# One quarter of the scan's inputs built by TensorE instead of GpSimd, with the scan tiles' partitions reordered and the schedule rewritten

## The chip, the cores and the metric

The kernel runs on one core of one Trainium2 chip. The metric is the device time of one execution in microseconds. The engines are named as in the profile: PE (TensorE; PEld is its weight loading), DVE (VectorE), ACT (ScalarE), POOL (GpSimd) and SP (SyncE, which here issues nearly all DMAs).

## The reference, cut to what matters

The input x is [32, 96, 56, 56]. Layer 0 is an inverted bottleneck of convolutions with a squeeze-and-excite gate; the change does not touch it. Layer 1 runs two Mamba blocks over the 3136 positions of each image, then a fusion, a batch norm and a residual. A Mamba block is:

```
xs, z = split(layernorm(seq) @ in_w)                # 192 channels each
xc    = silu(causal_conv(xs, 4 taps))
dt, B, C = split(xc @ xproj_w)                      # 6, 16 and 16 columns
delta = softplus(dt @ dt_w + dt_b)                  # [L, 192]
dA    = exp(delta[..., None] * A)                   # [L, 192, 16]
dBx   = delta[..., None] * B[:, :, None, :] * xc[..., None]
h     = scan: h_t = dA_t * h_(t-1) + dBx_t          # along L
y     = einsum('blds,bls->bld', h, C) + Dp * xc
out   = seq + (y * silu(z)) @ out_w
```

So each of 192 channels carries 16 states, and the largest arrays are dA, dBx and h with 192 x 16 rows of 3136 positions for each of 32 images and two blocks.

## The kernel before, in words

Layer 1 cuts each image into `NQ` = 4 chunks of `LC` = 784 positions: 128 chunks and two blocks, 256 *units* in all (`units`, L581). The work of a unit is `NT` = 24 *positions* `t`. At each position DVE scans a tile of 128 partitions x 784: 32 channels times 4 states. `place(t)` gives its block of 64 channels `k` (0 to 2), its group of four states `j` (0 to 3) and its half `p` of the block. The two positions with the same `k` and `j` are a *pair*; a unit has 12 pairs. A tile's partition is channel x 4 + state.

The main loop (the end of the phase, in `manual_schedule`) writes the order of all engines by hand. For each position `at` of the long sequence of 256 x 24 positions it emits, in this order:

- `inject(at + 4)`, once a pair: POOL multiplies u = delta * xc of the pair with B into `bx` (128 x 1568, L877), two pairs ahead of its scan;
- `decay(at + 1)`: ACT writes dA = exp(delta * A) (128 x 784, L857) into one of two PSUM buffers `da` of two banks each. So the exp for one position needs the buffer that the scan two positions earlier has given back;
- `bring(at)`, once a pair: ACT copies the first `LP` = 512 columns of C to PSUM as `cp` (L865);
- bursts in `early` (an activation that needs another function table: table load L590, the activation, table load back L591);
- `gated` (DVE, L941), `scan(at)` (DVE, L889), `product` (DVE multiplies h of the pair before by `cp`, columns 0 to 511, L897), `rest` (POOL does the other 272 columns, L904);
- `reduce(at - 5)`: PE sums h * C over the four states into `y` by matmuls with `rel` (L930);
- the steps that `prepare` and `finish` have put at this position: they make the inputs of the next unit (layer norm, the convolution by PE into `xs` L690, gate `z` L706, `bc` L715, `dt` L727, delta, u), and project a finished one (L789, L793);
- `fetch`: SP issues the loads that repeat rows over partitions, eight or nine positions ahead: delta and u (each row to 4 partitions) and B and C (4 rows to 32 channels each), all from scratch in DRAM that the unit's own steps have written (L722, L734).

Every engine works through its queue in this order, so a step of PE that waits holds up all PE work behind it. Banks for the steps' results come from a pool of two (`bank`), so a matmul step also waits until ACT or DVE has emptied the bank used two steps before. The delta activation (softplus), the silu of xc and the silu of z are three separate bursts in a unit. Block 1 works two chunks behind block 0 (`units`).

Of the kernel before, what the change touches and what calls it, by code (L numbers as in the profile page):

```python
# [11 lines left out]
F32 = mybir.dt.float32  # L12
# [15 lines left out]
LP = 512  # L28
# [9 lines left out]
ROUND = 12582912.0  # L38

# [14 lines left out]
def conv_mamba_kernel(ctx, tc, a, out):  # L54
# [397 lines left out]
    with ExitStack() as ph:  # L452
# [28 lines left out]
        v.tensor_reduce(rel, eye.rearrange("p (m s) -> p m s", s=SN), AX.X, ALU.add)  # L481
# [14 lines left out]
        move = once.tile([128, SG, DG, SN], F32, name="move", tag="move")  # L496
        v.tensor_copy(move, eye.rearrange("p (j s d) -> p j d s", j=SG, s=SN))
        acol = wts.tile([128, SG, NL, 2 * NB], F32, name="acol", tag="acolb")
        ps = bank("acol")
        for j in range(SG):  # L500
            for m in range(DB // DG):
                pe.matmul(
                    ps[m * 32 : m * 32 + 32, j * NL * 2 * NB : (j + 1) * NL * 2 * NB], move[:, j].rearrange("p d s -> p (d s)"),
                    araw[:, :, m :: DB // DG], start=True, stop=True,
                )
# [66 lines left out]
        g.memset(xn[C : C + 1, :], 1.0)  # L572
        tails = [wts.tile([C + 1, KC - 1], F32, name=f"tail{i}", tag=f"tail{i}") for i in range(NL)]
# [7 lines left out]
        units = [(0, 0), (1, 0)]  # L581
        for c in range(2, nch):
            units += [(c, 0), (c - 2, 1)]
        units += [(nch - 2, 1), (nch - 1, 1)]
# [3 lines left out]
        def through(t, func):  # L588

            s.activation(t, t, func)  # L590
            s.preload_act_table_set(MAIN)  # L591
# [6 lines left out]
        def prepare(n):  # L598
# [9 lines left out]
            def load():  # L608
                if i == 0:
                    seqs[c, 0] = wt([C, LC], "seq0", 3, n)  # L610
                    sp.dma_start(seqs[c, 0], x1d[b][:, q * LC : (q + 1) * LC])
# [5 lines left out]
            def square(h):  # L617
                if h == 0:
                    d["sq"] = wt([C, LC], "sq", 1, n)
                s.activation(d["sq"][:, cols(h)], d["cen", h][:C, :HB], AF.Square)  # L620
# [38 lines left out]
            def normalise(m):  # L659
                if m == 0:  # L660
                    d["xt"] = wt([TK, NK, C], "xt", 1, n)
                for k in TURNS[m]:
                    o = (k - TURNS[m][0]) * C
                    s.activation(d["xt"][:, k, :], d["ct", m][:TK, o : o + C], AF.Copy, scale=d["rs"][:, k : k + 1])  # L664
# [70 lines left out]

            def softplus():
                through(d["dl"], AF.Softplus)
                spread("delta", d["dl"], slice(0, NB))
# [16 lines left out]
            late, then = (9, 4) if n in (3, len(units) - 1) else (0, 0)  # L755
            steps = [(-4, load)]
            for h in range(2):
                steps += [(-1 + h + late, lambda h=h: center(h)), (-1 + 1 + h + late, lambda h=h: square(h))]
            steps += [(-1 + 2 + late, variance), (-1 + 3 + late, root), *[(t + late, lambda m=m: newton(m)) for m, t in enumerate((2, 2, 3))]]
            for h in range(2):  # L760
                steps += [(7 + h + then, lambda h=h: turn(h)), (8 + h + then, lambda h=h: normalise(h))]
                steps += [(9 + h + then, lambda h=h: turn_back(h)), (10 + h + then, lambda h=h: normal(h))]
            steps += [(11 + 3 + then, trail)]
            for k in range(NB):
                t = (12, 14, 16)[k] + then
                steps += [(t, lambda k=k: conv(k, (0, 1))), (t + 1, lambda k=k: conv(k, (2, 3)))]
                steps += [((14, 16, 18)[k] + then, lambda k=k: keep("xc", 3, "xs", k))]
            steps += [(18.5 + then, lambda: through(d["xc"], AF.Silu)), (20 + then, project_bc), (21 + then, store_bc)]
            for k in range(NB):
                steps += [((17, 19, 21)[k] + then, lambda k=k: gate(k)), ((18, 20, 22)[k] + then, lambda k=k: keep("z", 3, "zp", k))]  # L770
                steps += [((22, 22, 23)[k] + then, lambda k=k: project_dt(k)), ((23, 23, 24)[k] + then, lambda k=k: keep("dl", 1, "dtp", k))]
            steps += [(26.5 + then, lambda: through(d["z"], AF.Silu)), (34.5 + then, softplus), (35 + then, lambda: input_u(NB - 1))]
            steps += [(34 + then, lambda: bring_x(0)), (36 + then, lambda: input_u(0))]
            steps += [(38 + then, lambda: bring_x(1)), (39 + then, lambda: input_u(1))]
            return steps

        def finish(n):
# [17 lines left out]
            def store(h):  # L795
                if i + 1 < NL:
                    if h == 0:
                        seqs[c, i + 1] = wt([C, LC], f"seq{i + 1}", 3, n)
                    s.copy(seqs[c, i + 1][:, cols(h)], d["o", h][:C, :HB])
                    return  # L800
                if h == 0:
                    d["pre"] = wt([C, LC], "pre", 1, n)
                at = 2 * c + h
                s.activation(
                    d["pre"][:, cols(h)], d["o", h][:C, :HB], AF.Identity, bias=g2[:, b : b + 1],
                    accum_out=stats[:, 0, at : at + 1],
                )
                if at == 0:
                    s.activation(pivot, stats[:, 0, 0:1], AF.Copy, scale=-1.0 / HB)
                squares = wt([C, HB], "squares", 1, at)  # L810
                s.activation(squares, d["pre"][:, cols(h)], AF.Square, bias=pivot, accum_out=stats[:, 1, at : at + 1])

            def count():
# [5 lines left out]
                (4, lambda: [project(k) for k in (None, 0, 1)]), (5, lambda: project(2)),  # L819
                (6, lambda: store(0)), (7, lambda: store(1)), (8, count),  # L820
            ]

        LAG = 5
# [5 lines left out]
        def fetch(at, tags):  # L829

            n, t = divmod(at, NT)
            if not 0 <= n < len(units):
                return
            k, j, p = place(t)
            d = data[n]
            for tag in tags:
                if tag in ("delta", "u"):
                    if j == 0:
                        if p == 0:
                            d[tag, k] = wt([128, 2, LC], f"{tag}b", 2, f"{n}_{t}")  # L840
                        to = d[tag, k][:, p, :]
                        c0 = DB * (2 * k + p)
                        sp.dma_start(to, d[tag][c0 : c0 + DB, :].unsqueeze(1).to_broadcast([DB, SN, LC]))
                elif k == 0 and p == 0:
                    to = d[tag, j] = wt([128, LC], tag, 4 if tag == "B" else 5, f"{n}_{t}")
                    c0 = "BC".index(tag) * NS + j * SN
                    sp.dma_start(to, d["bc"][c0 : c0 + SN, :].unsqueeze(0).to_broadcast([DB, SN, LC]))

        das, bxs, hhs, hcs, cps, yps = {}, {}, {}, {}, {}, {}

        def decay(at):

            n, t = divmod(at, NT)
            i, d = units[n][1], data[n]
            k, j, p = place(t)
            das[at] = dpool.tile([128, 2 * 512], F32, name=f"da_{at}", tag="da")
            s.activation(das[at][:, :LC], d["delta", k][:, p, :], AF.Exp, scale=acol[:, j, i, 2 * k + p : 2 * k + p + 1])  # L857
# [13 lines left out]
        def inject(at):  # L871
# [3 lines left out]
            if p == 0:  # L875
# [5 lines left out]
        def scan(at):  # L881
# [4 lines left out]
            if p == 0:  # L886
                hhs[at] = wt([128, 2, LC], "hh", 3, at)
                hcs[at] = wt([128, 2, LC], "hc", 4, at)
            v.tensor_tensor_scan(  # L889
                hhs[at - p][:, p, :], das.pop(at)[:, :LC], bxs.pop(at), state[i][:, t : t + 1] if c % NQ else 0.0,  # L890
# [8 lines left out]
        def rest(at):  # L899
# [3 lines left out]
            if p == 1:  # L903
                g.tensor_mul(hcs[at - 1][:, :, LP:], hhs[at - 1][:, :, LP:], beside(data[n]["C", j][:, LP:]))  # L904
# [40 lines left out]
        for n in reversed(range(len(units))):  # L945
            for t, step in prepare(n):
                (todo if t % 1 == 0 else early).setdefault((n - 2) * NT + math.ceil(t), []).append(step)
            for t, step in finish(n):
                todo.setdefault((n + 1) * NT + t, []).append(step)

        s.preload_act_table_set(MAIN)
        with tc.manual_schedule():
            for at in range(min(todo), total + NT):
                if 0 <= at + 4 < total:
                    inject(at + 4)
                if 0 <= at + 1 < total:
                    decay(at + 1)
                if 0 <= at < total:
# [11 lines left out]
                if 0 <= at < total:  # L970
                    rest(at)
                if 0 <= at - LAG < total:
                    reduce(at - LAG)
                for step in todo.get(at, ()):
                    step()
                fetch(at + 8, ("delta", "u", "C"))
                fetch(at + 9, ("B",))

# [78 lines left out]
```

## Time and profile before

The times are 18930.19, 18954.67 and 18966.92 us, median 18954.67 us. The profiled execution spans 18935.6 us, which is 19 us (0.1%) below the median.

| what | value |
|---|---|
| span of the profiled execution | 18935.6 us |
| layer 1, from the first `y` matmul to the last | 3449.0 to 18640.9 us |
| DVE / POOL / ACT / PE busy share of the span | 93 / 81 / 77 / 79% |
| the same in layer 1 (8000 to 14000 us) | 98 / 99 / 86 / 78% |
| granted PE clock, whole span | 0.829 |
| DMA, mean | 140 GB/s; 0.51 of the engines' time in layer 1 |

How to read it: layer 0 takes the first fifth of the span and is not touched. In layer 1 the pattern of a unit repeats 256 times, so what counts is the time of one unit. A busy share is only a bound on how much an engine could be relieved; which engine is waited for is read from the waits. PE's busy time covers also the modelled tails of its matmuls and stretches at half clock, so it overstates how full PE is. A matmul of 32-bit numbers leaves two records in the trace.

### The profile page before, as it was taken

The page shows a single profiled execution, that of the slowest core. Times are in us where ns is not written, and L with a number is a line of the kernel's source. Part 1 is how long each engine was busy: PE and PEld are TensorE (multiplying, and loading weights), DVE is VectorE, ACT ScalarE, POOL GpSimd, SP SyncE. Part 2 cuts the span into 40 slices and gives each one's busy share as a digit, 9 for nine tenths or more (in the row PEclk, how much of TensorE's full clock was granted, in tenths as well). Part 3 has the DMA queues.
Part 4 walks back from the last instruction along what each step waited for, and adds up shares of the span by engine and source line. Part 5 has one row for each costly group of instructions (what it writes and reads, how often), then busy time and mean ns, then how long its engine had stood idle before and what let it go on. Part 6 is the DMA issues. An engine that isn't in the chain of part 4 may idle for free.

```text
span 18935.6 us, 291237 instructions
## 1 busy us (share of the span) xinstructions
PE 15002.3 (79%) x109276; PEld 6041.9 (32%) x109276; DVE 17699.9 (93%) x13147; ACT 14621.6 (77%) x24492; POOL 15355.8 (81%) x6638
## 2 busy tenths in 40 slices
PE   8999998777777777777777777777777777777772
PEld 4545444322222222222222222222222222222220
DVE  8888888799999999999999999999999999999993
ACT  4444444688888888888888888888888888888884
POOL 0000000799999999999999999999999999999994
PEclk9999999788888888888888888888888888888885
DMA  1010100455555554555555555555555555555557
GB/s 30 26 27 22 27 23 21 129 164 164 164 164 164 164 163 163 163 163 164 164 164 164 164 164 164 164 163 163 163 163 163 164 164 164 164 164 164 164 163 208
DMA packets 1049777, 2641.91 MB, mean 140 GB/s; under 512 B 130424, under 2 KB 343632, under 8 KB 1042216
## 3 DMA queue, kind: packets, MB, share of 16 engines
q1 hardware_dynamic: 1039720, 2584.68, 42.4%
q0 software_dynamic: 6656, 38.54, 1.0%
q8 instruction: 856, 14.02, 0.3%
q14 instruction: 561, 4.60, 0.1%
q10 hardware_dynamic: 1984, 0.07, 0.0%
HBM read 2172.52 MB, written 449.58 MB: 138 GB/s over the span
## 4 chain that ended last, share of the span: by engine, by line
issue 36%; DVE 27%; ACT 18%; PE 9%; POOL 7%; DMA 2%; SPq 0%; DVEq 0%; POOLq 0%; ACTq 0%
DVE hc L897 12%; DVE hh L889 12%; ACT da L857 5%; PE xs L690 5%; POOL bx L877 4%; ACT L590 3%; ACT L591 2%; DVE h L308 2%; ACT cp L865 2%; POOL hc L904 2%; DMA C<-bcd 1%; ACT z L590 1%; PE y L930 1%; ACT z L701 1%; ACT xc L590 1%
## 5 line engine op out<-in xcount | busy, mean ns | idle before, releaser
L877 POOL TENSOR_TENSOR bx<-ub,B 128x1568 f32<-128x1568 f32 x3072 | 10943.8, 3562 | 117.1 <-DMA ub<-ud 68.7
L889 DVE TENSOR_TENSOR_SCAN hh<-da,state,bx 128x784 f32<-128x784 f32 x4608 | 8301.2, 1836 | 196.1 <-ACT da L857 189.7
L857 ACT ACTIVATE da<-deltab,acol 128x784 f32<-128x784 f32 x6144 | 5592.6, 915 | 869.6 <-DVE hh L889 820.0
L904 POOL TENSOR_TENSOR hc<-hh,C 128x544 f32<-128x544 f32 x3072 | 4168.2, 1357 | 76.2 <-DVE hh L889 67.8
L690 PE MATMUL xs<-xn,wx 97*64 97x392 f32 x12288 | 2813.0, 611 | 1284.8 <-DVE us L751 1284.8
L897 DVE TENSOR_TENSOR hc<-hh,cp 128x1024 f32<-128x1024 f32 x3072 | 3669.0, 1194 | 0.1
L930 PE MATMUL y<-hc,rel 128*32 128x392 f32 x24576 | 2979.8, 568 | 29.0 <-DVE hc L897 17.3
L889 DVE TENSOR_TENSOR_SCAN hh<-da,bx 128x784 f32<-128x784 f32 x1536 | 2681.0, 1776 | 160.9 <-ACT da L857 145.9
L383 POOL TENSOR_TENSOR x<-x,x 96x784 f32<-96x784 f32 x128 | 286.3, 2237 | 3044.5 <-ACT x L382 2968.6
L308 DVE SCALAR_TENSOR_TENSOR h<-hpad,hp,h 128x1568 f32<-128x1568 f32 x1024 | 2036.5, 1989 | 34.2
L690 PEld LDWEIGHTS xs<-xn,wx 97*64 97x64 f32 x12288 | 995.6, 165 | 3074.3 <-DVE us L751 1531.9
L865 ACT COPY cp<-C 128x512 f32<-128x512 f32 x3072 | 1784.7, 581 | 230.4 <-DVE hc L897 207.9
L715 PE MATMUL bc<-xc,wbc 64*64 64x392 f32 x3072 | 878.1, 728 | 542.5 <-ACT xc L590 542.5
L282 PE MATMUL dw<-hpad,diag 32*32 32x392 f32 x36864 | 1101.0, 514 | 46.9 <-issue 45.9
L671 PE MATMUL xn<-eye,xt 112*96 112x112 f32 (+1 forms) x4096 | 743.6, 350 | 433.6 <-ACT xt L664 432.3
L701 ACT COPY xc<-xs 128x392 f32<-128x392 f32 x768 | 372.1, 485 | 915.6 <-PE xs L690 915.6
L930 PEld LDWEIGHTS y<-hc,rel 128*32 128x32 f32 x24576 | 542.0, 114 | 1456.1 <-issue 1287.7
L590 ACT ACT_TABLE_LOAD x768 | 985.3, 1283 | 13.5
L591 ACT ACT_TABLE_LOAD x768 | 985.3, 1283 | 11.3
L380 PE MATMUL c<-h,w3s 128*96 128x392 f32 (+1 forms) x2560 | 958.3, 519 | 36.9 <-DVE w3s L365 36.9
L793 PE MATMUL o<-z,outw 64*96 64x392 f32 x3072 | 862.4, 699 | 96.4 <-DVE z L941 96.2
L289 ACT ACTIVATE h<-dw,turn 128x392 f32<-128x392 f32 x512 | 340.1, 673 | 731.8 <-PE dw L282 731.8
(172 smaller groups left out, 17257.0 us busy)
## 6 DMA issues: line engine op xcount, KB each, us to landing
deltab<-deltad SPq DMA_DIRECT2D x1536, 392.0 KB, 5.7
ub<-ud SPq DMA_DIRECT2D x1536, 392.0 KB, 5.9
B<-bcd SPq DMA_DIRECT2D x1024, 392.0 KB, 6.8
C<-bcd SPq DMA_DIRECT2D x1024, 392.0 KB, 5.2
deltad<-dl SPq DMA_DIRECT2D x512, 294.0 KB, 3.4
ud<-us SPq DMA_DIRECT2D x512, 196.0 KB, 2.8
ud<-us SPq DMA_DIRECT2D x512, 98.0 KB, 2.9
x<-in_x_dram SPq DMA_DIRECT2D x32, 1176.0 KB, 7.7
```

The source lines that it names most:

```text
L282: pe.matmul(ps[r][to : to + 32, :HB], diag[src, n, t, :], hb[src, r0 : r0 + RB, dx : dx + W], start=t == 0, stop=t == 8, skip_group_check= ...
L308: v.scalar_tensor_tensor(acc, src, tap, acc, ALU.mult, ALU.add)
L590: s.activation(t, t, func)
L591: s.preload_act_table_set(MAIN)
L690: pe.matmul(d["xs", k][h * 64 : h * 64 + 64, :HB], wx[:, i, o, k * 64 : k * 64 + 64], xn[:, o + h * HB : o + h * HB + HB], start=o == 0, s ...
L857: s.activation(das[at][:, :LC], d["delta", k][:, p, :], AF.Exp, scale=acol[:, j, i, 2 * k + p : 2 * k + p + 1])
L865: s.copy(cps[at], data[n]["C", j][:, :LP])
L877: g.tensor_mul(bx, data[n]["u", k], beside(data[n]["B", j]))
L889: v.tensor_tensor_scan(hhs[at - p][:, p, :], das.pop(at)[:, :LC], bxs.pop(at), state[i][:, t : t + 1] if c % NQ else 0.0, ALU.mult, ALU.add,)
L897: v.tensor_mul(hcs[at - 1][:, :, :LP], hhs[at - 1][:, :, :LP], beside(cps.pop(at)))
L904: g.tensor_mul(hcs[at - 1][:, :, LP:], hhs[at - 1][:, :, LP:], beside(data[n]["C", j][:, LP:]))
L930: pe.matmul(yps[k][r0 : r0 + DB, :HB], rel, hc[:, p, h * HB : h * HB + HB], start=False, stop=j == SG - 1, skip_group_check=True,)
```

## The change

Of the four groups of states, group `PEJ` = 0 is no longer multiplied by POOL. For the 6 positions of a unit with `j` = 0, PE forms delta * xc * B as a matrix product: u, transposed so that sequence positions lie on partitions (`turn_u`, `keep_u`), times a matrix that has B of one state on its diagonal (`fill`). 784 columns are done as 8 blocks of 120 or 91 columns, and each of the four states goes to its own 32 partitions of PSUM, 32 small matmuls a position. For that the tile's partition order becomes state x 32 + channel, which changes the loads' broadcasts, `rel` and `acol`.

The diagonal matrices come through DRAM: two buffers `bdiag` are filled with zeros once; in each unit `turn_b` and `diagonal` write B's values into one of them with a row pitch that is two elements longer than the row that is later read, so that they land on a diagonal; one load brings the 120 x 3144 matrix (1.5 MB) to SBUF (`fetch` of `diag`).

The products lie in the PSUM buffers that `da` has otherwise; the exp of these positions goes to SBUF instead, into slots of `bx` (`lend`), and is made three or four positions ahead (one or two at the start of a unit). B of group 0 is not loaded any more. `LP` goes from 512 to 400, so DVE takes 400 columns of h * C and POOL 384.

The silu of xc and of z become one burst at the scan of `t` = 15, softplus is the burst at `t` = 7: each just before a pair with `j` = 0. All steps of `prepare` and `finish` get new places with fractions that order them within a position. Block 1 of a chunk now comes `BACK` = 3 chunks behind. Buffers shrink (`hc` 4 to 3, `B` 4 to 3, `C` 5 to 4, `sq` and `xt` in one tag), `LAG` is 4, and `squares` is written to PSUM.

The diff, cut to its core:

```diff
-LP = 512
+LP = 400
+PEJ = 0
+TB = 120
+TOFF, TCOL, TSZ = (0, 120, 211, 301), (0, 120, 211, 302), (120, 91, 91, 91)
+TW = TCOL[-1] + TSZ[-1]
+TR = 8 * TW
...
+        none = once.tile([TB, TR + 2], F32, name="none", tag="none")
+        v.memset(none, 0.0)
...
+        for t in bdiag:
+            sp.dma_start(t.rearrange("(p r) -> p r", p=TB), none)
...
+            def turn_b():
+                ps = d["bt"] = bank(f"bt_{n}")
+                for b in range(4):
+                    pe.matmul(
+                        ps[: TSZ[b], b * 2 * SN : (b + 1) * 2 * SN], d["bcs"][:, TOFF[b] : TOFF[b] + TSZ[b]],
+                        bsel.rearrange("p h s -> p (h s)"), start=True, stop=True,
+                    )
+            def diagonal():
+                bt = wt([TB, 4, 2, SN], "bt", 1, n)
...
+                s.copy(bt[:, 0], ps[:TB, 0])
+                s.copy(bt[:z, 1:], ps[:z, 1:])
...
+                for h in range(2):
+                    sp.dma_start(to[:, :, h, :2], bt[:, 0, h].rearrange("p (e s) -> p e s", e=2))
+                    for e in range(2):
+                        sp.dma_start(
...
+            def turn_u(k):
+                ps = d["utp", k] = bank(f"ut_{n}_{k}")
+                for b in range(4):
+                    pe.transpose(ps[: TSZ[b], b * 128 : b * 128 + 128], d["us"][:, k, TOFF[b] : TOFF[b] + TSZ[b]], eye)
+            def keep_u(k):
...
+                s.copy(ut[:, 0], ps[:TB, 0])
+                s.copy(ut[:z, 1:], ps[:z, 1:])
...
-            steps += [(18.5 + then, lambda: through(d["xc"], AF.Silu)), (20 + then, project_bc), (21 + then, store_bc)]
-            steps += [(26.5 + then, lambda: through(d["z"], AF.Silu)), (34.5 + then, softplus), (35 + then, lambda: input_u(NB - 1))]
+            steps += [(17.5, project_bc), (18.1, store_bc), (18.5, turn_b), (19.1, diagonal)]
+                steps += [((38.6, 46.6, 52.6)[k], lambda k=k: turn_u(k)), ((39.2, 47.2, 53.05)[k], lambda k=k: keep_u(k))]
+            bursts = [(15, lambda: through([d["xc"], d["z"]], AF.Silu)), (31, softplus)]
...
-        LAG = 5
+        LAG = 4
...
+        def lend(at):
+            if by_pe(at) and at % 2 == 0:
+                to = wt([128, 2, LC], "bx", 3, at)
+                for p in range(2):
+                    das[at + p] = to[:, p, :]
...
+        def fill(at):
...
+            ps = dpool.tile([128, 2 * 512], F32, name=f"bp_{at}", tag="da")
+            bxs[at] = ps[:, :LC]
+            dg = d["diag"].rearrange("p (e h x s) -> p e h x s", e=2, h=2, s=2)
+            for h in range(2):
+                for b in range(4):
+                    z, o, x = TSZ[b], h * HB + TOFF[b], TCOL[b]
+                    for sg in range(SN):
+                        pe.matmul(
+                            ps[sg * DB : sg * DB + DB, o : o + z], d["ut", k][:z, b, h, p * DB : p * DB + DB],
+                            dg[:z, sg // 2, h, x : x + z, sg % 2], start=True, stop=True, skip_group_check=True,
+                        )
...
-            if p == 0:
+            if p == 0 and j != PEJ:
                 bx = wt([128, 2, LC], "bx", 3, at)
                 g.tensor_mul(bx, data[n]["u", k], beside(data[n]["B", j]))
...
-                if 0 <= at + 1 < total:
+                if 0 <= at + 1 < total and not by_pe(at + 1):
                     decay(at + 1)
+                for x in range(at, at + 5):
+                    pair = x // 2 * 2
+                    if 0 <= x < total and by_pe(x) and pair - ahead(pair)[x - pair] == at:
+                        decay(x)
...
                 if 0 <= at < total:
                     rest(at)
+                if 0 <= at + 1 < total and by_pe(at + 1):
+                    fill(at + 1)
                 if 0 <= at - LAG < total:
                     reduce(at - LAG)
...
-                fetch(at + 8, ("delta", "u", "C"))
+                fetch(at + 9, ("delta",))
+                fetch(at + 8, ("u",))
                 fetch(at + 9, ("B",))
+                fetch(at + 5, ("C",))
+                fetch(at + 7, ("diag",))
```

In the new order a `fill` stands at the positions `t` = 23, 0, 7, 8, 15 and 16 of a unit (for 0, 1, 8, 9, 16 and 17). At these six, apart from the `y` matmuls, PE has no other step ordered.

## Prediction

> **What bounds the kernel now.** I read the page first (busy shares), then the busy time in the steady stretch 8000 to 14000 us, the groups of instructions in it, the list of waits in it, and last single microseconds of PE. The busy-time view of the stretch (columns: length, then busy us of PE, PEld, DVE, ACT and POOL, each with its instructions in brackets; granted PE clock, DMA share, GB/s), beside layer 0 and two short pieces:
>
> ```profile
> 0.00:3640.00 3640.00, 3304.39 (x44776) 1733.11 (x44776) 3044.19 (x2020) 1652.57 (x2649) 479.44 (x225) 0.93 0.12 34
> 8000.00:14000.00 6000.00, 4692.99 (x25898) 1730.05 (x25896) 5862.29 (x4451) 5159.22 (x8746) 5939.89 (x2555) 0.81 0.51 163
> 10004.00:10013.00 9.00, 8.21 (x28) 2.44 (x28) 8.58 (x9) 6.71 (x15) 9.00 (x5) 0.50 0.35 90
> 10016.00:10023.00 7.00, 6.95 (x50) 2.01 (x48) 6.15 (x5) 5.63 (x10) 7.00 (x3) 1.00 0.99 318
> ```
>
> The groups of instructions of the same stretch:
>
> ```profile
> L877 POOL TENSOR_TENSOR bx<-ub,B 128x1568 f32<-128x1568 f32 x1215 | 4324.7, 3559 | 36.4 <-DMA ub<-ud 18.4 <-POOL hc L904 10.9 <-issue 6.5
> L889 DVE TENSOR_TENSOR_SCAN hh<-da,state,bx 128x784 f32<-128x784 f32 x1828 | 3292.8, 1836 | 76.4 <-ACT da L857 74.3 <-issue 0.2
> L857 ACT ACTIVATE da<-deltab,acol 128x784 f32<-128x784 f32 x2427 | 2209.1, 915 | 325.7 <-DVE hh L889 305.4
> L904 POOL TENSOR_TENSOR hc<-hh,C 128x544 f32<-128x544 f32 x1214 | 1642.6, 1353 | 23.7 <-DVE hh L889 21.6
> L897 DVE TENSOR_TENSOR hc<-hh,cp 128x1024 f32<-128x1024 f32 x1214 | 1450.0, 1194 | 0.0
> L865 ACT COPY cp<-C 128x512 f32<-128x512 f32 x1213 | 704.6, 581 | 89.7 <-DVE hc L897 80.8
> L590 ACT ACT_TABLE_LOAD x304 | 390.0, 1283 | 5.4
> L751 DVE TENSOR_TENSOR us<-dl,up 128x392 f32<-128x392 f32 x202 | 110.0, 545 | 0.0
> ```
>
> 1214 pairs are 101.2 units, so a unit takes 6000 / 101.2 = **59.3 us**; all 256 would take 15180, and layer 1's `y` matmuls span 15192. Per unit POOL is busy 58.7, DVE 57.9, ACT 51.0, PE 46.4. POOL and DVE bound the unit together; POOL idles 0.6 us and DVE 1.4. The list of waits says whom DVE waits for, and that PE's large waits are its own:
>
> ```profile
> PEld xs L690 <- DVE us L751: 613.5, 101, 6.9
> DVE hh L889 <- ACT da L857: 132.1, 240, 1.6
> ```
>
> 132.1 / 101.2 = 1.3 us a unit: nearly all of DVE's idle time is waiting for the exp, up to 1.6 us at once (behind the three activation bursts). Relieving POOL alone would be worth at most 1.4 us a unit; POOL and DVE must both become shorter.
>
> **POOL and DVE after.** POOL loses 3 of 12 multiplications by B: 3 x 3.56 = 10.7 us. Its share of h * C grows from 544 to 768 elements a pair; the slope between its two rows is (3559 - 1353) / 1024 = 2.15 ns an element, so +0.48 us x 12 = 5.8. POOL: 58.7 - 10.7 + 5.8 = 53.8. DVE's product shrinks from 1024 to 800 elements; slope between 1194 (1024 elements) and 545 (392) 1.03 ns, so 0.23 us x 12 = 2.8 less. DVE: 57.9 - 2.8 = **55.1**. Scans keep one operand in SBUF and one in PSUM, with roles swapped in one quarter: nothing. So DVE becomes the bound, with POOL 1.3 us below. POOL's work is now lumpy: 3.56 + 1.84 = 5.4 us in three pairs, 1.84 in the fourth, against about 4.6 of DVE. It falls back 0.8 a pair, 2.5 in all, and regains it in the fourth; since it multiplies two pairs (over 9 us) ahead, the scan isn't late.
>
> **ACT.** Bursts: six table loads become four, -2 x 1.28 = -2.6 us. `cp` of 400 columns: about 0.09 less x 12 = -1.1. New: per unit three pairs of transposed copies, by the neighbouring ACT copies (0.48 for 392 columns, 0.19 for the 2-column state copy) about 0.75 a pair, +2.3; two small copies of B, +0.4. ACT stays at 50 us. The exp of a `j` = 0 pair is made ahead into SBUF and the bursts (silu 1.28 + 1.18 + 1.18 + 1.28 = 4.9 us, softplus 3.7) stand just before such a pair, so DVE has two scans and a product (2 x 1.79 + 0.97 = 4.6) that need no exp. The silu burst with its neighbours is longer than that by up to about 1 us. I keep DVE's idle time at 0.4 to 1.5, value 1.2: it was 1.3, the longest single cover improves, and new waits come in. Unit: 55.1 + 1.2 = **56.3 us**.
>
> **PE, the new work.** A fill is 32 matmuls, 64 records, in rounds of four (one to each 32 columns of the array): 16 rounds of about 98 columns. The nearest row is `y`, also four side by side; here warm, and at half clock:
>
> ```profile
> 10016.23 0.86 PE L930 MATMUL y<-hc,rel 128*32 128x392 f32 x8
> ...
> 10056.51 1.54 PE L930 MATMUL y<-hc,rel 128*32 128x392 f32 x8
> ```
>
> Eight records of about 0.51 us in 0.86 are two rounds 0.35 apart, or 0.89 ns a column; so 98 columns cost 0.087 a round, 1.4 a fill. Lower bound. Weight loading may set the pace: the `ct` step's loads of 112 weight columns follow at 98 ns,
>
> ```profile
> 10049.74 0.86 PEld L657 LDWEIGHTS ct<-cen,seq 96*112 96x112 f32 x8 [0.79 <-ACT seq L799]
> ```
>
> ((0.86 - 0.18) / 7), so 32 columns cost 28 ns, four of them 0.11 a round, 1.8 us a fill if they go one after another under the matmuls. I take 1.8; with 0.1 to start and the 0.26 of a short matmul's end (`ct`), a fill is ready 2.15 us after its buffer came free. It has a product and a scan of DVE for that, 0.97 + 1.79 = 2.75 us: **hidden by 0.6**. The Trainium skill ("TensorE: Matmul & The Clock Gate", Part 3, The mechanism) speaks against it: weight loads overlap running matmuls only when their row groups differ, and here every load uses all rows. By that a round is 0.087 + 0.11, a fill 3.15 us, ready at 3.5, late by 0.75; six fills, 4.5 us a unit, would eat the whole gain of 3.0 and make the kernel 400 us slower. The row decides against the rule: `y` uses all 128 rows too, and its second round starts 0.35 after the first, where exposed loads would put it at 0.46; in `ct` loading and multiplying in turn would take twice 98 ns. I leave it as part of a rival.
>
> Per unit PE gets 6 x 1.8 = 10.8 us, 12 transposes (24 records of 128 columns, 0.11 each) 2.6, and the turned B 0.3: **+13.7 us**. Now 46.4 busy at a mean clock of 0.81 is 37.7 at full clock; after, 51.4 of 56.3. That fits only while the clock is full. The same page (Part 1) says an idle window of about 3.4 us halves the clock. The trace agrees: PE stood nearly 5 us behind `us`, then ran at 0.50 from 10004 to 10013. In layer 0, busy 91%, the clock is 0.93, so more work brings more clock: 51.4 / 0.93 = 55.3, still under 56.3, barely. At the six positions with fills no other PE steps but `y` are ordered, so no large batch stands ahead of a fill; what would be late behind a blocked fill is its scan, then all of DVE.
>
> **DMA and SP.** Gone: one B load, 128 rows at the usual 392 KB. New: the 1.5 MB diagonal matrix, about four such loads, and 6 small stores of 8-byte runs. Net +3 loads on some 25 of that size, DMA share 0.51 to about 0.6. The diagonal load waits for the fill of `t` = 17, goes out at position 17 and is wanted at 23, 14 us later, where such loads land in 5 to 7 us; the matrix at 318 GB/s needs 4.7 by itself and behind the delta, u and B loads of its neighbours some 10. C now goes out 6 positions (14 us) ahead instead of 9. Hidden; if not, PE's fill for `t` = 0 or the copy `cp` is late, then DVE. SP's stores wait on ACT's copies of B, with B and C loads queued behind them, which have 5 to 6 positions. The added issues, 6 net at about 0.6 us, cost SP 4 us of 56 that it has.
>
> **Start and end.** Zeroing and storing the two matrices (3 MB) and more small matmuls for `acol`, and a longer run-up: +20 us (0 to 40), once.
>
> **Sum.** (59.3 - 56.3) x 256 = 768 less, +20: 18935.6 - 748 = 18188 against the profiled span; the median stands 19 higher: 18207. I say **18210 us**, 3.9% less. The likeliest case's own range: DVE idle 0.4 gives -973 + 0 = 17980; 1.5 with +40 gives 18300, and with the odd late fill 18420.
>
> **Rivals.** (1) Some fills come late, with the gain halved: in the trace about one `y` round in six runs at half clock (0.65 instead of 0.35, as in the second `y` line). A fill then is ready at about 4.1 if loading slows too, 1.3 late; one or two of a unit's six so cost 1.3 or 2.6 us a unit: 18540 to 18870, value 18600. For: half clock is over a third of today's time (mean 0.81). Against: idle stretches that cause it are what PE now has less of. (2) The other side: PE becomes the bound. If its clock stays at 0.81, 51.4 / 0.81 = 63.5 us a unit, (63.5 - 59.3) x 256 = 1075 slower: 20050. It decides below a clock of 51.4 / 59.3 = 0.87. For: PE runs its queue in order and waits in it. Against: 37.7 counts modelled tails, and layer 0's 0.93. The rule on weight loads above would be this side's milder form (19360). (3) It does less than it says: POOL falls behind and DVE waits for `bx`, or a late diagonal load costs 1.5 us a unit: 18600; against it speaks the lead of two pairs.
>
> **How the numbers follow.** Likeliest case 0.64, (1) 0.14, (2) 0.12, (3) 0.10. The likeliest gives the time. Low end 17950 (DVE's floor of 55.1 with idle 0.3); the high end takes in (1) and (3): 18700; left out are (2) and a tail. A difference under 0.2% (38 us) can't be told from none, as the three runs before differ by that much. Faster 0.85: the likeliest, and (1) and (3) but for 0.03; same 0.02; slower 0.13.
>
> **What would show it.** Right: `bx` on POOL 9 a unit at 3.56; `hc` on POOL near 1.84 and on DVE near 0.97; DVE over 97% busy in layer 1, units of 56.3; fills of 64 records within 1.9 us; a clock above 0.9; four table loads a unit. Wrong: DVE's `hh` waiting for PE's `bp` by more than 1 us a unit, PE over 95% busy, fills of 3 us, or a clock still near 0.8.

## The result and the profile after

The changed kernel takes **28126.0 us** (28099.74 to 28174.4, four runs), against 18954.4 us for the kernel before on the same chip: a ratio of 1.4847 (interval 1.4826 to 1.4868). The prediction was 18210 us. It was wrong in sign and far outside its range of 17950 to 18700.

The busy-time view of a steady stretch of the changed kernel (columns as in the prediction: length, busy us of PE, PEld, DVE, ACT and POOL, granted PE clock, DMA share, GB/s):

```profile
12000.00:20000.00 8000.00, 5287.09 (x55412) 2622.74 (x55416) 4722.53 (x3696) 4093.35 (x7757) 4541.00 (x1870) 0.75 0.37 114
```

From the first scan to the last a unit takes 95.1 us (59.4 before). Per unit POOL is busy 4541.00 / 8000 x 95.1 = 54.0 us, DVE 56.1, ACT 48.7. So each vector engine does about what the prediction worked out (53.8, 55.1, about 50), and then stands idle 40 us. DMA moves 114 GB/s where it moved 163, at a share of 0.37 where it was 0.51 and 0.6 was expected. The page's chain (share of the span by engine, then by line) and groups say what all wait for:

```profile
DMA 53%; issue 12%; SPq 11%; PE 7%; POOL 6%; ACT 6%; DVE 4%; POOLq 0%; DVEq 0%; ACTq 0%
...
L966 POOL TENSOR_TENSOR bx<-ub,B 128x1568 f32<-128x1568 f32 x2304 | 8113.0, 3521 | 6604.6 <-DMA B<-bcd 3366.0
L993 POOL TENSOR_TENSOR hc<-hh,C 128x768 f32<-128x768 f32 x3072 | 5574.3, 1815 | 3940.9 <-DMA C<-bcd 1919.0
...
L985 DVE TENSOR_TENSOR hc<-hh,cp 128x800 f32<-128x800 f32 x3072 | 2976.2, 969 | 3135.9 <-ACT cp L954 3133.9
...
L954 ACT COPY cp<-C 128x400 f32<-128x400 f32 x3072 | 1505.2, 490 | 5374.8 <-DMA C<-bcd 5223.2
L943 PE MATMUL bp<-diag,ut 91*32 91x91 f32 (+1 forms) x98304 | 3041.3, 283 | 1380.9 <-DMA diag<-bdiag 1365.8
```

The third column is the idle time ahead of each group with its releaser. The largest releaser is a load in four of these five rows, and in the fifth (DVE behind `cp`) the copy that itself waits for a load. A chain with 53% of the span in DMA at a DMA share of 0.37 means that the loads are slow, not that the engines for them are full. The timeline of SP shows how they are slow. Two lines of the kernel before:

```profile
10013.80 0.55 SPq L847 DMA_DIRECT2D B<-bcd  x1
10014.83 0.56 SPq L843 DMA_DIRECT2D deltab<-deltad  x1
```

and the changed one:

```profile
15003.00 3.74 SPq L907 DMA_DIRECT2D C<-bcd  x1
15006.79 3.83 SPq L899 DMA_DIRECT2D deltab<-deltad  x1
15010.68 7.54 SPq L899 DMA_DIRECT2D ub<-ud  x2
15018.33 3.74 SPq L907 DMA_DIRECT2D C<-bcd  x1
...
15033.86 1.72 PE L943 MATMUL bp<-diag,ut 120*32 120x120 f32 x64
```

Issuing a load of 392 KB took 0.55 us; now, in a backlog, SP is held 3.74 us by each. In the trace's DMA packets 4.1 of the 16 DMA engines are busy from 15002 to 15038 us, with packets of 3136 bytes at 127 ns: 392 KB in 3.74 us is 107 GB/s. In the kernel before such loads came in bursts on 15 or more engines. A unit has 6 loads of delta, 6 of u, 4 of C and 3 of B: 19 x 3.74 = 71 us on four engines. Counted from the packets between 12000 and 19500 us, packets of 3136 bytes (nearly all of them these loads) are under way in 85 of a unit's 95 us, in 76 of them four or five at a time. The diagonal matrix moves for 14 us, all but 4 of them beside such loads. So for 89 of 95 us the unit's loads are on their way.

What changed is the order in which a load repeats its rows. Before, the slowest dimension of the source's access pattern was 32 channels (`DB`); after, it is 4 states (`SN`; `to_broadcast([SN, DB, LC])`, L899 and L907). The Trainium skill ("DMA: Bandwidth & Descriptors", Why a DMA increments its semaphore by 16 and not by 1) says that a DMA is spread over the largest number of engines, up to 16, that divides the slowest dimension of both its sides; its Rules for kernel authors say that an outermost dimension under 16, such as a leading repeat of few copies, confines the DMA to at most that many engines. The destination here has 128 partitions, the source 4 states. That gives 4 engines, and the trace shows 4.1 busy.

The last line of the timeline above is a fill. It takes what was predicted (1.72 us against 1.8).

### The profile page after: what moved, and what is told of

It is laid out like the page before. It is cut to its first block, busy times and chain, and to the rows that moved or that the text cites. A ratio compares the mean times of both kernels' runs of the same rounds, so it can differ in the third digit from the quotient of the medians.

```text
span 28132.7 us, 502070 instructions
## 1 busy us (share of the span) xinstructions
PE 19191.6 (68%) x212796; PEld 9654.0 (34%) x212796; DVE 17265.5 (61%) x13151; ACT 14037.6 (50%) x26028; POOL 14147.0 (50%) x5870
## 4 chain that ended last, share of the span: by engine, by line
DMA 53%; issue 12%; SPq 11%; PE 7%; POOL 6%; ACT 6%; DVE 4%; POOLq 0%; DVEq 0%; ACTq 0%
DMA C<-bcd 18%; DMA diag<-bdiag 18%; SPq L899 10%; DMA B<-bcd 7%; DMA seq<-out_dram 5%; POOL bx L966 5%; PE bp L943 2%; DMA ub<-ud 2%; DVE h L314 2%; PE cen L637 2%; DMA deltab<-deltad 1%; POOL hc L993 1%; ACT L612 1%; DVE hh L977 1%; ACT L613 1%
## 5 line engine op out<-in xcount | busy, mean ns | idle before, releaser
L966 POOL TENSOR_TENSOR bx<-ub,B 128x1568 f32<-128x1568 f32 x2304 | 8113.0, 3521 | 6604.6 <-DMA B<-bcd 3366.0
L993 POOL TENSOR_TENSOR hc<-hh,C 128x768 f32<-128x768 f32 x3072 | 5574.3, 1815 | 3940.9 <-DMA C<-bcd 1919.0
L977 DVE TENSOR_TENSOR_SCAN hh<-da,state,bx 128x784 f32<-128x784 f32 x3456 | 6329.9, 1841 | 1398.9 <-ACT da L929 1390.9
L929 ACT ACTIVATE da<-deltab,acol 128x784 f32<-128x784 f32 x4608 | 4203.5, 916 | 2840.8 <-DVE hh L977 2738.6
L985 DVE TENSOR_TENSOR hc<-hh,cp 128x800 f32<-128x800 f32 x3072 | 2976.2, 969 | 3135.9 <-ACT cp L954 3133.9
L977 DVE TENSOR_TENSOR_SCAN hh<-bx,state,bp 128x784 f32<-128x784 f32 x1152 | 2124.9, 1845 | 3612.4 <-PE bp L943 3601.8
L954 ACT COPY cp<-C 128x400 f32<-128x400 f32 x3072 | 1505.2, 490 | 5374.8 <-DMA C<-bcd 5223.2
L943 PE MATMUL bp<-diag,ut 91*32 91x91 f32 (+1 forms) x98304 | 3041.3, 283 | 1380.9 <-DMA diag<-bdiag 1365.8
L943 PEld LDWEIGHTS bp<-diag,ut 91*32 91x32 f32 (+1 forms) x98304 | 2802.0, 126 | 2085.6 <-issue 2035.1
L929 ACT ACTIVATE bx<-deltab,acol 128x784 f32<-128x784 f32 x1536 | 1443.3, 940 | 2137.5 <-DMA deltab<-deltad 2137.5
```

The source lines that it names most:

```text
L929: s.activation(das[at], d["delta", k][:, p, :], AF.Exp, scale=acol[:, j, i, 2 * k + p : 2 * k + p + 1])
L943: pe.matmul(ps[sg * DB : sg * DB + DB, o : o + z], d["ut", k][:z, b, h, p * DB : p * DB + DB], dg[:z, sg // 2, h, x : x + z, sg % 2], star ...
L954: s.copy(cps[at], data[n]["C", j][:, :LP])
L966: g.tensor_mul(bx, data[n]["u", k], beside(data[n]["B", j]))
L977: v.tensor_tensor_scan(hhs[at - p][:, p, :], das.pop(at), bxs.pop(at), state[i][:, t : t + 1] if c % NQ else 0.0, ALU.mult, ALU.add,)
L985: v.tensor_mul(hcs[at - 1][:, :, :LP], hhs[at - 1][:, :, :LP], beside(cps.pop(at)))
```

## Experiments: the loads

The theory, A in the expectations: the loads' order costs the time. The rivals put the loss on the fills or the diagonals, or on the new schedule. The units below are the time from the first scan to the last through 256; idle times of VectorE are means over units, by the position of the scan that they precede.

**The new order alone.** The kernel before with the partition order of the changed one (loads, `rel`, `acol`) and nothing else:

```diff
-sp.dma_start(to, d[tag][c0 : c0 + DB, :].unsqueeze(1).to_broadcast([DB, SN, LC]))
+sp.dma_start(to, d[tag][c0 : c0 + DB, :].unsqueeze(0).to_broadcast([SN, DB, LC]))
-sp.dma_start(to, d["bc"][c0 : c0 + SN, :].unsqueeze(0).to_broadcast([DB, SN, LC]))
+sp.dma_start(to, d["bc"][c0 : c0 + SN, :].unsqueeze(1).to_broadcast([SN, DB, LC]))
```

> The kernel before with nothing changed but the partition order of the scan tiles (state outside channel): the loads of delta, u, B and C repeat 4 blocks of 32 rows, the outermost dimension of the source is 4, and rel and acol are permuted to match. No matrix product, no diagonal, old schedule. Theory A (such a load runs on 4 of the 16 DMA engines, 3.74 us for 392 KB): 20 loads a unit are 75 us of DMA one after another, with the stores some 80, so a unit takes 75 to 82 us instead of 59.3: 22900 to 24800 us. Rival B (the 8-byte stores and the 1.5 MB diagonal load hold the queue up): stays at 18950 us. Rival C (the fills or the new places of the steps hold DVE up): 18950 us.

Measured 27857 us, ratio 1.4701 (1.4671 to 1.473), a unit of 94.0 us. Busy times and two of the largest waits of a stretch:

```profile
10000.00:16000.00 6000.00, 3320.45 (x16347) 1220.96 (x16346) 3750.74 (x2811) 3280.81 (x5528) 3747.32 (x1614) 0.68 0.29 103
```

```profile
POOL bx L881 <- DMA ub<-ud: 1861.3, 128, 15.8
DVE hh L893 <- POOL bx L881: 1816.0, 238, 15.4
```

No diagonal, no fill, no new schedule, and a loss of 8903 us where the whole change lost 9172. Theory A holds, and the rivals fall as the cause of this loss. The parts do not simply add up: the fills come back below as a second cause, which shows only once the loads are fast. The time lies over A's 22900 to 24800, which counted the transfers alone. Packets of 3136 bytes are under way in 82.5 of a unit's 94 us, about what A has, and in the other 11.5 there are none. SP's being held (16% of this run's chain is SP's queue) is a likely reason for those, not shown to be all of it.

**Loads back on 16 engines.** First B and C: each row is stored four times in DRAM, so that 16 rows stand outermost.

```diff
-d["bc"] = udram.tile([2 * NS, LC], ...)
+d["bc"] = udram.tile([2 * NS, 4, LC], ...)
...
-sp.dma_start(to, d["bc"][c0 : c0 + SN, :].unsqueeze(1).to_broadcast([SN, DB, LC]))
+rows = d["bc"][c0 : c0 + SN].rearrange("s r l -> (s r) l")
+sp.dma_start(to, rows.unsqueeze(1).to_broadcast([4 * SN, DB // 4, LC]))
```

> The changed kernel, but B and C are stored four times a row in DRAM, so that their loads have 16 rows outermost; delta and u keep 4. Theory A: 7 loads a unit go from 3.74 to about 1.1 us, 95.0 - 19 = 76 us a unit, about 23300 us; delta and u still at 3.7 us an issue. Rivals B and C: 28100 us within 2%.

Measured 23933.6 us (1.263), a unit of 78.7, 630 us over A's figure and far from the rivals'. Then also delta and u, each in four loads of 32 rows:

```diff
-sp.dma_start(to, d[tag][c0 : c0 + DB, :].unsqueeze(0).to_broadcast([SN, DB, LC]))
+for sg in range(SN):
+    sp.dma_start(to[sg * DB : sg * DB + DB], d[tag][c0 : c0 + DB, :])
```

> As the run before, and each load of delta and u in four of 32 rows (98 KB), so that no load has 4 outermost. Theory A: the sum of the prediction applies, 18200 us, if SP can issue some 71 DMAs a unit at about 0.55 us (39 of 56 us); up to 18900 if that makes loads late. Rival B: the diagonal load and the 8-byte stores alone still hold the queue, over 21000 us. Rival C: over 21000 us, with DVE waiting for the products of PE.

Measured 20427.6 us, ratio 1.0774 (1.0756 to 1.0792), a unit of 64.9: 7698 us of the loss are back. The time is over A's 18200 to 18900 and under the 21000 of both rivals: something besides the loads costs time here, and what VectorE now waits for is what rival C names, the products of TensorE (next section).

**The price of this repair, and the order alone again.** The new partition order with these loads, in the kernel before:

> The kernel before with the new partition order, but with loads that keep 16 or 32 rows outermost: B and C stored four times a row, delta and u loaded in four pieces. Theory A (the outermost 4 is the whole cost of the order): back at 18950 us within 2%, against 27857 with the order alone. If the order costs something else (the other read pattern, the permuted weights), above 19500 us.

Measured 19369.8 us, ratio 1.0224 (1.0203 to 1.0244). The loads on four engines cost 27857 - 19370 = 8487 us in this kernel. The 2.2% that remain lie between the two forecasts (under 19330, over 19500); how much of them is the four issues for one, the copies in DRAM or the order itself isn't separated.

**The loads as they were.** To be rid of the repair's price too, the changed kernel with the access patterns of before; the rows then lie in other partitions than the arithmetic wants, so it sums other rows, with the same instructions:

> The changed kernel with the loads of delta, u, B and C as the kernel before had them (channels outermost, one load each on all 16 engines); all else, the fill and its order included, as changed. It leaves out that the loaded rows lie where the arithmetic wants them: the sums are over other rows than the reference's. If the loads' order alone made the prediction wrong, this is the prediction, a unit of 56.3 us and 18200 us. If the fills' place in TensorE's queue costs what the run with all loads on 16 engines showed (a unit of 64.9, of which the split loads had cost 1.6 in the kernel before), it is 62 to 64.5 us a unit, 19700 to 20300 us, with 7 to 9 us of idle VectorE a unit ahead of the scans of positions 0, 8 and 16.

Measured 20363.9 us, ratio 1.0743 (1.0725 to 1.0761):

```profile
10000.00:16000.00 6000.00, 5202.43 (x61038) 2588.25 (x61038) 5122.38 (x4068) 4536.51 (x8573) 5002.87 (x2056) 0.86 0.57 168
```

The time is 64 us over the second forecast, and far from the 18200 of the first. So in the changed kernel the split loads cost 64 us, no more, and with the loads of before it is still 7.4% slower than before: there is a second cause, worth about 2150 us against the prediction. VectorE idles 9.4 us a unit where the prediction took 1.2; 8.2 x 256 = 2100 us is that.

## Experiments: the fills' place in the queue

In the run with all loads on 16 engines the same stretch reads

```profile
10000.00:16000.00 6000.00, 5184.26 (x60743) 2573.61 (x60739) 5102.93 (x4054) 4515.55 (x8532) 4980.40 (x2049) 0.86 0.68 171
```

DVE is busy 5102.93 / 6000 x 64.9 = 55.2 us a unit, the predicted floor, and idle 9.6, of it 2.9, 2.7 and 2.4 us ahead of the scans of positions 0, 8 and 16: the first of each pair that TensorE fills. The list of waits of this stretch (92.4 units) names the fill first, and POOL second:

```profile
DVE hh L981 <- PE bp L947: 484.4, 178, 4.7
DVE hh L981 <- POOL hc L997: 200.9, 67, 3.3
```

The timeline ahead of position 8:

```profile
12031.52 1.56 PE L848 MATMUL o<-seq,fusw 96*96 96x392 f32 x4 [0.91 <-ACT ut L793]
...
12033.01 2.22 PE L852 MATMUL o<-z,outw 64*96 64x392 f32 x12
...
12035.16 1.70 PE L947 MATMUL bp<-diag,ut 120*32 120x120 f32 x64
...
12036.98 1.85 DVE L981 TENSOR_TENSOR_SCAN hh<-bx,state,bp 128x784 f32<-128x784 f32 x1 [1.27 <-POOL bx L970]
```

(The trace names POOL's `bx` as the releaser of that scan; that ended at 12036.89, and the fill's last matmuls are as late.) The fill is what the scan waits for: over 200 units these three scans start 0.11 to 0.18 us after the end of their fill in nine cases of ten, while POOL's last instruction ended anywhere up to 1.8 us earlier. The fill is ordered behind the output projection, which had waited for a bank that ScalarE was to empty. Over 200 units the first fill of a pair starts 3.2 to 3.8 us after its buffer is free, with TensorE busy all that time, issues its 64 records in 1.4 us, and the scan starts 0.4 us after the last of them. The fill is as fast as predicted, and late. What makes it late was tried in several ways.

**Less work on TensorE.** The run with 16-engine loads, leaving out the `y` sums of 9 of the 12 pairs:

> The changed kernel with the 16-wide loads, leaving out 9 of the 12 y sums of a unit (only the last group of states is summed), which takes 6 to 8 us of matmuls off PE, spread over all positions. In the kernel with the y sums PE starts the first fill of a pair 3.2 to 3.8 us after its buffer came free and is busy all that time. Theory F (a backlog of work ahead of the fill): the backlog shrinks by 2 us or so at each of three places, 59 to 61 us a unit, 18800 to 19400 us. Rival G (round trips between PE and ACT through the two banks set the start, whatever PE has to do): within 1 us a unit of 64.9, over 20150 us.

Measured 20277.2 us (1.0698), a unit of 64.5. A quarter of the `y` work is left, and 0.45 us a unit is gained, as rival G forecast and theory F did not. The run does not separate the two cleanly, though. Less work came with a lower clock (0.80 in this stretch, 0.86 with all sums): a matmul of the output projection (L852) took 720 ns instead of 647, and TensorE's wait for ScalarE ahead of that projection (L848) grew from 2.2 to 3.4 us a unit. The first fill started 0.8 us earlier at position 0 but 1.0 us later at position 8. So taking work off TensorE is no remedy by itself; that it has time enough for all of it is shown only by the last run below, which does all its steps in a unit of 58.8 us.

**A shorter fill.** Fills that use 32 of the 91 to 120 rows of a diagonal, leaving out the other rows' products:

> The same, with all y sums, but the fill uses only 32 rows of its diagonal and runs up to eight matmuls side by side, leaving out the rest of the sum: 0.8 to 0.9 instead of 1.4 us a fill, in the same place with the same waits. If the length of the fill is what is late: 0.5 us less for each of three to six fills, 61.9 to 63.4 us a unit, 19650 to 20050 us. If it is the start alone that matters little: 20400 us.

Measured 20194.3 us (1.0655), a unit of 64.1, between the two forecasts. The fills of positions 0, 8 and 16 issue in 0.94 instead of 1.43 us and start as late as before. The waits ahead of these three scans shrink by 1.7 us together, as three fills 0.5 shorter would have it; half of that comes back at other positions, and 6.3 of the 8.0 us stay. The fill's own length is the smaller part.

**A fill ordered earlier.** The first fill of a pair at the end of the scan that frees its buffer, ahead of that position's other steps:

```diff
-if 0 <= at + 1 < total and by_pe(at + 1):
+if 0 <= at + 2 < total and at % 2 == 0 and by_pe(at + 2):
+    fill(at + 2)
+if 0 <= at + 1 < total and at % 2 == 0 and by_pe(at + 1):
     fill(at + 1)
```

> The changed kernel with the 16-wide loads, and the fill of a pair's first position put one position earlier in PE's queue, ahead of the steps of that position. What is left over the sum there is 8.6 us a unit, of which DVE idles 8.1 before the scans of t = 0, 8 and 16. Theory D (PE reaches the first fill late because steps that wait for ACT's emptying of the two banks stand ahead): a good part of the 8.1 goes, 19000 to 19800 us. Rival E (PE is simply full, 56 of 65 us busy): no gain, 20400 us.

Measured 20141.2 us (1.0631), a unit of 64.0: 1.0 us a unit, over D's 19000 to 19800 and a little under E's 20400, so by itself no verdict for either. The idle time ahead of positions 0, 8 and 16 fell from 8.0 to 5.3 us, and 1.6 of it came back ahead of 1, 9 and 17. And with the output projection a position later besides:

> As the run before, with the output projection of the finished unit (3.6 us of PE) one position later, behind the fill for t = 8. Theory D: the idle time before t = 8, 2.7 us a unit, goes as well: some 500 us less than the run before, 18600 to 19400 us. Rival E: 20400 us as before.

Measured 21200.6 us (1.1189), worse by 1059 and against both forecasts. The idle time ahead of position 8 went (2.1 to 0.4), and 6.3 us came ahead of position 9, where the projection now stood before the second fill. A step isn't moved out of the way by moving it behind the next.

**Steps moved one by one.** On the fill-first kernel: the transposes of u for blocks 1 and 2 to positions 16 and 0, a convolution closed one position earlier, the gates one to three earlier.

> The version with the first fill one position earlier (20141 us), and with steps moved so that fewer wait for ACT ahead of a fill: the transposes of k = 1 and 2 to positions 16 and 0, the second convolution closed one position earlier, two of three gate steps earlier. All steps and results kept. If PE's waiting for the banks ahead of t = 8 and 16 (2.1 us before t = 8) makes the backlog: 2 to 4 us a unit less than 63.8, 19100 to 19650 us. If not: 20100 us or more.

Measured 19734.0 us (1.0411), a unit of 62.4, 84 us over the forecast for waits of banks. Then the Newton steps on VectorE, the two bursts, the delta projections, and the projection of B and C with all behind it:

> The kernel of the run before (all loads on 16 engines, first fill of a pair one position earlier, transposes and gates moved), and four more moves of layer 1's steps, all results kept: the three Newton steps on VectorE one position later, the silu burst at position 14 for 15 and softplus at 30 for 31, the projection of B and C, its turn and the diagonals some 0.8 positions earlier, the delta projections up to 1 position earlier. The run before has a unit of 62.4 us with 6.9 us of idle VectorE: 1.7 before the Newton steps, 1.2 at position 10, 1.5 at 17 and 18, 1.9 at 0 and 1. If the idle time is a matter of where ScalarE and TensorE steps stand in their queues, 2 to 5 us of it go: a unit of 57.5 to 60.5, 18500 to 19250 us. If each step that is moved only meets its partner's wait elsewhere, as when the output projection was moved, it stays at 19600 to 20000.

Measured 20680.8 us (1.0908), slower by 947, where neither forecast had it. The list of waits names the cause:

```profile
PE bp L947 <- DMA diag<-bdiag: 374.1, 91, 6.8
```

The store of B and C had come to stand ahead of the diagonals' load on SP's queue, where it waits for the projection; the load goes out late and the fill of position 0 waits 4.1 us. With the store, and what follows from it, behind that load again (`(18.05, store_bc)` for `(17.2, store_bc)`):

> The kernel of the run before (20681 us) with one step back: the store of B and C, and with it their turn and the diagonals, are ordered behind the load of the diagonals at position 17, as in the kernel before it, while the projection and the other moves stay. In the run before, the store (ordered at 17.2, waiting for the projection) stood ahead of the diagonals' load on SP's queue, and TensorE waited for that load 4.1 us in most units. If that wait is what made it slower, some 4 us a unit go: 19350 to 19650 us, near the 19734 or a little under it. If the other moves made it slower, it stays at 20400 to 20700.

Measured 19416.0 us (1.0242), as forecast: 1265 us back, a little more than the wait's 4.1 x 256 = 1050. Here 5.6 us of idle time a unit are left, 2.0 directly ahead of the scan of position 17 and 1.6 ahead of the gate's product that follows the scan of 19. The timeline at position 17:

```profile
13067.31 0.90 PE L637 MATMUL cen<-seq,cen 96*96 96x392 f32 x2
...
13069.09 0.65 PE L786 MATMUL ut<-eye,us 128*120 128x128 f32 x4 [0.89 <-ACT sx L642]
...
13070.36 1.67 PE L947 MATMUL bp<-diag,ut 120*32 120x120 f32 x64
...
13072.07 1.79 DVE L981 TENSOR_TENSOR_SCAN hh<-bx,bp 128x784 f32<-128x784 f32 x1 [1.62 <-PE bp L947]
```

A transpose that waits 0.89 us for its bank stands ahead of the fill. Two positions later with it:

```diff
-((38.6, 40.6, 48.6)[k], lambda k=k: turn_u(k)), ((39.2, 41.02, 49.02)[k], lambda k=k: keep_u(k))
+((40.6, 42.6, 48.6)[k], lambda k=k: turn_u(k)), ((41.02, 43.1, 49.02)[k], lambda k=k: keep_u(k))
```

> The kernel of the run before (19416 us; 5.6 us of idle VectorE a unit, of them 2.0 at position 17 and 1.6 ahead of the gates' product at 19) with one move: the turns of u of the first two blocks two positions later (16.6 and 18.6 for 14.6 and 16.6). In the run before, the turn at 14.6 stood ahead of the fill of position 17 on TensorE and waited 0.9 us for the squares of ScalarE, and took 0.65 us. If places in TensorE's queue are the cause, 1.0 to 1.6 us of the 2.0 at position 17 go: 19000 to 19180 us. If the wait only moves to another position, it stays within 80 us of 19416.

Measured 19270.2 us (1.0167), a unit of 60.5. The wait at position 17 fell to 0.1 us as expected, but that of the gate's product rose from 1.6 to 3.2: of 1.9 us a unit 0.6 was gained in the end, and the time lies between the two forecasts. With the steps ahead of the `y` sums moved as well (variance and root one position later, the turn of B 0.85, the first delta projection 1.0):

> The kernel with the later turns, and besides: the variance with its root one position later, the turn of B 0.85 and the first delta projection one position later, so that the y sums of position 17 and 18 no longer stand behind them on TensorE. Ahead of it the product of gate and y (position 19) waited 1.6 us a unit. If places in the queue are the cause, 1.2 to 1.6 us a unit more go: 18600 to 18850 us, a little under the kernel before. If the wait moves to the Newton steps or to the delta projections, it stays at 19000 to 19400.

Measured **18821.5 us** (18789.0 to 18846.8), ratio **0.9925** (0.9908 to 0.9941), as forecast: this version is 0.7% faster than the kernel before, where the prediction had 3.9%.

```profile
10000.00:16000.00 6000.00, 5445.10 (x67298) 2670.42 (x67292) 5656.80 (x4481) 4970.31 (x9416) 5507.06 (x2266) 0.93 0.74 190
```

A unit takes 58.8 us; per unit DVE is busy 55.4, POOL 54.0, ACT 48.7, PE 53.4 at a clock of 0.93. VectorE idles 3.3 us, of it 1.2 ahead of the gate's product that follows the scan of position 3 and 0.5 behind the scan of 16. The first fills of positions 0, 8 and 16 start 0.9, 0.1 and 0.7 us after their buffers are free, where they started 3.7, 3.6 and 3.3 us after in the run with all loads on 16 engines: with the same steps and the same arithmetic, their place made them late. Of the nine runs of this section only this one and the one with the store met a forecast of the theory of places; it rests on the single moves whose waits could be followed, not on its figures. So nothing in the change itself keeps it slower than the kernel before; the places of its steps did. In the kernel before POOL is busy 58.7 of 59.4 us, so a better order could have given that kernel at most 0.7 us a unit, 180 us or 0.9%. The version here gains 0.7% and still has 3.3 us of idle time; that a retuned kernel before couldn't match it was not tried.

## Why the prediction was wrong, point by point

- **DMA and SP: the step that failed.** It counted bytes and the number of issues, and took landing times and 0.6 us an issue from the loads of the kernel before, though the change turns those loads' access pattern round. They went from 16 engines to 4. "Hidden" cost 28126 - 20364 = 7760 us by the run with the old loads. The rivals had no such case: (3) had a late diagonal load at 1.5 us a unit, not 19 slow loads. The rule stands in the page named above; the 4 stood in the new `to_broadcast` lines.
- **"No large batch stands ahead of a fill": the second that failed.** It read only which steps are ordered at the six positions; what the positions before leave undone still stands in the queue, as in the projection above. The sum had the fill start 0.1 us after its buffer is free; it starts 3.2 to 3.8 us after. With that 0.6 us of cover becomes 2.4 to 2.9 us of delay, three times a unit. Rival (1) named late fills but a wrong reason, fills at half clock (they issue in 1.4 us), and priced 1.3 to 2.6 us a unit; it was 8.2. Moving steps alone, from the run with all loads on 16 engines to the last one, won 1606 us of it back.
- **The fill's own price: right.** 1.4 us to issue (taken 1.8, lower bound 1.4 from the `y` row). The rule of the Trainium skill ("TensorE: Matmul & The Clock Gate", Part 3, The mechanism) that weight loads overlap only between different row groups would have made it 3.15, by the prediction's estimate from it; these loads use 91 to 120 of 128 rows and follow at 22 ns a record all the same; no run shows the rule. Row over rule was the right choice.
- **POOL and DVE: right.** `hc` on POOL 1.815 us (1.84 predicted), on DVE 0.969 (0.97), `bx` 3.52; per unit POOL 54.0 (53.8), DVE 55.2 to 55.4 (55.1) once loads are fast. DVE's idle time of 1.2 was wrong in every run: about 39 with the slow loads, 9.4 with those of before, at best 3.3.
- **PE and its clock: right only for the reordered version.** There PE is busy 53.4 of 58.8 us, 91%, at 0.93: the pair that layer 0 shows, from which the sum took 55.3 at 0.93. In the changed kernel, where PE waits for loads, the clock is 0.75, and with the loads of before it is 0.86, under the 0.9 that the prediction named. Rival (2), PE as the bound, didn't come.
- **Start and end:** the span less the stretch of the scans is 3735 us before, 3784 after, 3789 in the last version: +49 to +54, not +20 (0 to 40).

## What to carry to other kernels

When a change reorders partitions, look at the slowest dimension of every load that feeds them, in source and destination, before anything else: the same bytes can go out on a quarter of the DMA engines, and the issuing queue is then held as well. For a step that must be on time, what counts is the work ordered ahead of it on its engine, with the waits inside that work, not what shares its position. Move one such step at a time and read where the wait comes out; a move that passes another engine's or SP's waiting instruction can cost more than it frees.

## What was not expected of the hardware

- A load of 128 rows of 3136 bytes on four DMA engines: 3.74 us, 107 GB/s, and in a backlog SP is held 3.74 us an issue instead of 0.55.
- The stores of 8-byte runs for the diagonals are cheap: 1572 packets a unit at about 9 ns, 14 us of one engine's time.
- 64 weight loads of 32 columns, each with its matmul, issue in 1.4 us: 22 ns a record. That is what the matmuls' columns alone would take by the `y` row (1.4 us), so the loads cost nothing beside them.
- Taking away three quarters of the `y` sums lowered the mean clock of PE from 0.866 to 0.816.
